# Wide fp32 products of a cross attention kernel as four strips of 32 columns, with a redrawn order of tasks

## The chip, the cores and the metric

The kernel runs on one core of one Trainium2 chip. The metric is the device time of one execution in microseconds (us); 602.05 us is the median of three runs before the change. The engines of the core are TensorE (PE; its weight loads are shown apart as PEld), VectorE (DVE), ScalarE (ACT), GpSimd (POOL) and SyncE (SP), which issues nearly all DMAs.

## The reference, cut to what matters

All arrays are fp32. `x` is (2, 2048, 640), the context (2, 128, 384): its first 124 tokens are text, the last 4 are `ca`.

```python
query = x @ Wq;  keyt = enc @ Wk;  valt = enc @ Wv           # enc: the first 124 tokens
hs = mha(query, keyt, valt)                                  # 8 heads of 80
ca_q1 = einsum('btc,th->bch', ca, Wq_ca)[:, indices, :]      # 384 rows, spread to 2048 by indices
ca_hs1 = mha(ca_q1, x, x)
ca_hs2 = mha(ca_hs1 @ Wq, ca @ Wk_ca, ca @ Wv_ca)
out = (hs + ca_hs2) @ Wout + b_out + x
```

## The kernel before, in words

The order of all work is made by a planner written in the kernel, the class `Desk`. Each piece of work is a Python generator (a task) that yields operations `Do(engine, fn, after, needs, ..., rank, mode)`. `Desk.run` keeps a clock for each engine. Among the operations whose events have come and whose rooms (PSUM banks, buffers) are free, it takes for each engine those that can start first, and of these the one with the lowest sum of rank, a correction of its task from the table `RANKS`, and `change(mode)`, a price for leaving the tiling in which TensorE is. `issue` then emits the instructions, and the planner's own durations (`START`, `DRAIN`, `DRAINS` for TensorE) advance the clock. The instructions are pinned in the order in which they were emitted. So the tables set the order of the program; they cost nothing at run time.

Most TensorE work passes through `Desk.matmul` (L212), which emits one instruction for each product, and `Desk.transpose` (L222). An fp32 product shows as two matmul records and two weight loads. TensorE works in these tilings, written rows*columns of the array:

- 128*128, whole: the wide products. `queries`, `queries_fast` with its inner task `chain`, and `plain` make the queries (`pq<-xt,wq_sb`, `pq<-x_sums,wq_sums` and kin) out of blocks of 512 rows of `x`; a second inner task named `chain`, in `text_out_fast`, multiplies by Wout (`po<-wout_sums,hs`, `po<-wout_sb,hs` and kin, 320 columns). Both use sums of blocks, so that seven block products stand for eight. Smaller ones: `pk`, `pv`, `pw`, `po<-w_sb,p2T`. The transposes (`pt_...`, `pm`) are whole too.
- 128*32, four strips side by side: `hidden` (`ph<-pT,vpad`, values by probabilities) and `contract` (`acc<-ea,y_sb`).
- 64*128: `text_scores` (`sc<-kmain,q`, `sc<-krest,rests`) and half of `yz_block` (`pyz`).
- 32*128, four row groups: the adapter's scores (`s<-zop,cop` for the maxima, `s<-cop,zop` for the exponentials).

Operations of the wide chains carry `mode=(P, P)`, `sc` carries `(64, P)`, `ph` carries `(P, 32)`; the others carry none, and their change costs nothing in the planner's choice. `idle_work` multiplies zeros at the start, 14 times.

Around the products: `softmax` takes the maxima of `sc` on VectorE (`m`), the exponentials on ScalarE (`p`), the division on POOL or VectorE, a block transpose on VectorE (`eb`), and a DMA round trip through HBM (`kept`, then `pT`). The adapter's maxima (`mx`) are on VectorE, its exponentials (`ea`) on ScalarE. Queries are read out of PSUM by ScalarE and VectorE (`q`), and each `po` is added to rows of `x` by VectorE (`x_more`, `last_rows`); `stored` sends these rows out, with the adapter's part added by an indirect DMA that POOL issues. There are 8 blocks of 512 rows and 16 units `m` of 256 rows.

In the chains a product waits for the read of the same PSUM bank before it: `yield Do("PE", product, ready + at, needs=needs, mode=(P, P))`, where `at` is the event of that read.

Of the kernel before, what the change touches and what calls it, by code (L numbers as in the profile page):

```python
# [14 lines left out]
P = 128  # L15
# [4 lines left out]
class Event:  # L20


    def __init__(self):
        self.t = None
# [33 lines left out]


class Task:  # L60
    def __init__(self, gen, rank, key, more):
        self.gen, self.rank, self.key, self.more, self.last = gen, rank, key, more, Event()


class Desk:
# [1 line left out]


    ENGINES = ("PE", "ACT", "DVE", "POOL", "SP", "NONE")
    WHOLE, SWITCH, LEAVE, ANOTHER = (P, P), 12.6, 12.9, -0.8  # L70
    START = {(P, P): 0.107, (64, P): 0.143, (P, 64): 0.107, (64, 32): 0.1, (P, 32): 0.03}
    DRAIN = {
        ((P, P), (32, P)): 0.136, ((P, P), (64, P)): 0.035, ((P, P), (P, 64)): 0.056, ((P, P), (P, 32)): 0.067,
        ((32, P), (P, 32)): 0.049, ((P, 64), (P, P)): 0.07, ((P, P), (P, P)): 0.0,
    }
    DRAINS = {(64, P): 0.172, (32, P): 0.108, (P, 32): 0.115}
    MORE = {
        "v_transpose": 0.025, "v_stream_shuffle": 0.09, "v_scalar_tensor_tensor": 0.07, "v_reciprocal": 0.035,
        "a_activation": 0.045,
# [3 lines left out]


    RANKS = {
        "adapter": {1: 0.3},
        "chain": {8: -11, 9: -18, 12: -2, 13: -1, 14: -17, 15: -5, 17: 4, 18: 4, 19: 8, 20: -6, 24: -15, 26: 6,
            27: 2, 37: -13, 38: 14, 39: 14, 40: 14, 41: 3, 45: 6, 50: 12, 51: 10, 52: -5, 57: -2, 62: 2, 65: -8,
            67: 0.1, 68: 0.1, 69: 0.1, 71: 11, 80: -12, 85: 9},
        "contract": {0: 4, 3: 8},  # L90
        "halves_away": {1: -6, 6: 7},
        "keys": {0: 4},
        "probabilities": {3: 7, 4: 1, 8: -4, 10: 4, 14: -0.5},
        "queries": {0: -2},
        "queries_fast": {4: 1},
        "residual": {14: -14},
        "rest_back": {8: 4, 9: 12, 10: -11},
        "second": {0: 1.6},
        "softmax": {12: -6, 19: 4, 21: 1, 22: 3, 23: -3, 24: 2, 26: -7, 27: -10, 28: 10},
        "stored": {7: -8},  # L100
        "sums_of_wq": {0: 4},
        "text_scores": {0: -2, 5: -2},
        "text_values": {0: 13},
        "values_weights": {0: 6},
        "wq_turned": {0: 2},
        "x_load": {1: -12, 6: -6},
        "y_rows": {1: 5, 3: 10, 4: 10, 7: 10},
        "yz_block": {0: -11, 1: -6, 5: 1.3, 6: 5, 7: 4.7},
    }

    def __init__(self, tc):
        self.tc, self.nc, self.now, self.spent, self.mode = tc, tc.nc, 0.0, 0.0, None
        self.free = {e: 0.0 for e in self.ENGINES}
        self.queue = {e: [] for e in self.ENGINES}
        self.events, self.landed, self.channel, self.log, self.begun = {}, 0.0, 0.0, [], {}

    def event(self, key):
        return key if isinstance(key, Event) else self.events.setdefault(key, Event())
# [2 lines left out]
        return self.event(key).t is not None  # L121

    def begin(self, gen, rank):
        name = gen.__name__
        n = self.begun[name] = self.begun.get(name, -1) + 1
        task = Task(gen, rank, (name, n), self.RANKS.get(name, {}).get(n, 0.0))
        task.last.t = self.now
        self.go_on(task, None)

# [16 lines left out]
    def change(self, mode):  # L146


        if mode is None or mode == self.mode:
            return 0.0  # L150
        return self.LEAVE if self.mode == self.WHOLE else self.SWITCH if mode == self.WHOLE else self.ANOTHER

    def order(self, op):
        return (op.order() if callable(op.order) else op.order) + op.task.more
# [55 lines left out]
        self.mode, self.idle = mode, False  # L210

    def matmul(self, out, lhsT, rhs, **kw):  # L212
        self.pin(self.nc.tensor.matmul(out, lhsT, rhs, **kw))  # L213
        n = 1
        for size in rhs.shape[1:]:
            n *= size
        self._mode(*lhsT.shape)
        at_once = (P // self.mode[0]) * (P // self.mode[1])
        one = lhsT.dtype == F32R
        self.spent += self.slow() * (1 if one else 2) * max(n / 1.2, 107) / 1e3 / at_once  # L220

    def transpose(self, out, in_, ident):  # L222
        self.pin(self.nc.tensor.transpose(out, in_, ident))
# [41 lines left out]
def kernel(  # L265
# [40 lines left out]
    desk = Desk(tc)  # L306
# [217 lines left out]
    def idle_work():  # L524

        zeros = sp.tile([P, P], F32, name="zeros")
        yield Do("DVE", lambda: desk.v_memset(zeros, 0.0), [])

        op = yield Do("NONE", lambda at: (bank(at[0], "unread"), at[0]), needs=[(banks, 1)])
        to, at = op.value
        for n in range(IDLE):

            def product():
                matmul(to[:, :P], zeros, zeros, start=True, stop=True)

            yield Do("PE", product, [] if n else [op.at], frees=[(banks, at)] if n == IDLE - 1 else [])

# [559 lines left out]
    def queries(n, after, first=False):  # L1099

        b, sb = divmod(n, NSB)
        yield Do("NONE", lambda: None, after)
        t, at = xt[b, sb]

        def room(s):
            q_of[n] = q_slot(s[0], f"q_{n}"), s[0]

        if first:
            yield Do("NONE", room, after, needs=[(qslots, 1)])
            q = q_of[n][0]  # L1110
            op = yield Do("NONE", lambda s: [bank(i, f"pq_{n}_{c}") for c, i in enumerate(s)], [], needs=[(banks, 3)])
            pq, three = op.value, op.slots[0]
            for i in range(NCH):

                def part(i=i):
                    for c in range(3):
                        matmul(
                            pq[c], wq_of(i, c), t[:, :, i, :], start=(i == 0), stop=(i == NCH - 1)
                        )

                op = yield Do("PE", part, [*after, ("wq", i)])
            for c in range(3):
                yield Fork(one(evacuate(q[:, c, :], pq[c], three[c], after=[op.at], marks=[("qc", n, c)])), 4)
        for c in range(3 if first else 0, NCH):

            def part(s, z=None, c=c):
                if z:
                    room(z)
                pq = bank(s[0], f"pq_{n}_{c}")
                for i in range(2):  # L1130
                    matmul(pq, wq_of(i, c), t[:, :, i, :], start=(i == 0), stop=False)
                return pq

            own = [(qslots, 1)] if n not in q_of else []
            op = yield Do("PE", part, [*after, "wq4"], needs=[(banks, 1), *own], mode=(P, P))
            pq, s, q = op.value, op.slots[0][0], q_of[n][0]

            for i0, i1 in ((2, 4), (4, NCH)):

                def part(c=c, i0=i0, i1=i1):  # L1140
                    for i in range(i0, i1):
                        matmul(pq, wq_of(i, c), t[:, :, i, :], start=False, stop=(i == NCH - 1))

                op = yield Do("PE", part, mode=(P, P))
            if c < 4:
                yield Fork(one(evacuate(q[:, c, :], pq, s, after=[op.at], marks=[("qc", n, c)], rank=0)), 0)
            else:
                yield Fork(halves_away(n, pq, s, op.at) if n else first_halves(pq, s, op.at), 0)
        used(b, sb, op)
        yield Do("NONE", lambda: None, [("qc", n, c) for c in range(4)], marks=[("q", n)])  # L1150
# [49 lines left out]
    def queries_fast(n, after):  # L1200
# [28 lines left out]
                if n + 1 == len(blocks):  # L1229
                    desk.event("last query").t = op.at.t  # L1230

        def chain(c, steps):

            po, s, at = None, None, []
            for k, ((x, y, plus), ready, (i, u)) in enumerate(steps):
# [19 lines left out]

                if x is not None:
                    needs = ([(banks, 1)] if k == 0 else []) + ([(qslots, 1)] if n not in q_of else [])
                    op = yield Do("PE", product, ready + at, needs=needs, mode=(P, P))
                    if k == 0:
                        po, s = op.value, op.slots[0][0]  # L1260
                    if n not in forked:
                        forked.add(n)
                        desk.event(("q slot", n)).t = desk.now
                        for c2 in (1, 2, 3):
                            yield Fork(chain(c2, chains[c2]), rank + 0.1 * c2)
                if plus:
                    op = yield Do("PE", fifth, [op.at] + at, mode=(P, P))
                counted(op, any(key[0] == "xs" for key in ready))
                yield from read(i, u, po, s, op.at, k == len(steps) - 1)
                at = [desk.event(("qr", n, i, u, len(begun_of[n, i, u]) - 1))]  # L1270
# [14 lines left out]
                    frees=frees, marks=marks, rank=0,  # L1285
                )), 0)

        yield Fork(chain(0, chains[0]), rank)
        yield Do("NONE", lambda: None, [("q slot", n)])
        yield from plain(n, t, NCH - 1, rank - 0.5, counted)  # L1290
        yield Do(
# [7 lines left out]
    def plain(n, t, c, rank, counted):  # L1299
# [4 lines left out]
                matmul(pq, wq_of(i, c), t[:, :, i, :], start=(i == 0), stop=False)  # L1304
            return pq

        op = yield Do("PE", part, needs=[(banks, 1)], mode=(P, P), rank=rank)
        pq, s = op.value, op.slots[0][0]
        for i0, i1 in ((2, 4), (4, NCH)):

# [1 line left out]
                for i in range(i0, i1):  # L1312
                    matmul(pq, wq_of(i, c), t[:, :, i, :], start=False, stop=(i == NCH - 1))

            op = yield Do("PE", part, mode=(P, P), rank=rank)
        counted(op, False)
        yield Fork(halves_away(n, pq, s, op.at), 0)

# [726 lines left out]
    def text_out_fast(m, rank):  # L2045
# [51 lines left out]
            (((s4, w[1][1], (0, 1)), [("hs", m, "s4")] + end_h, ((0, 1),)),),  # L2097
        )

        def chain(n, steps):  # L2100

            po, s, at = None, None, []
            for k, ((x, y, plus), after, ((i, u),)) in enumerate(steps):

                def product(s=None, k=k, x=x, y=y, plus=plus):
# [9 lines left out]
                    return to  # L2115

                op = yield Do(
                    "PE", product, after + at + ready, needs=[(banks, 1)] if k == 0 else [], mode=(P, P), rank=rank
                )
                if k == 0:  # L2120
                    po, s = op.value, op.slots[0][0]
# [15 lines left out]
                    yield Fork(stored(m, i, ends[m, i]), 1)  # L2137

        for n, steps in enumerate(chains):
            yield Fork(chain(n, steps), 30 + m)  # L2140

    fast_of, tile_left, ends = {}, {}, {}

# [109 lines left out]
```

## Time and profile before

| what | value |
|---|---|
| median of 3 runs | 602.05 us (601.88 to 604.86) |
| profiled execution: span from first to last instruction | 600.3 us |
| TensorE busy, matmul records | 583.0 us, 4535 |
| VectorE / ScalarE / POOL busy | 404.1 / 282.2 / 151.1 us |
| DMA moved | 113.55 MB, mean 189 GB/s |

The profile gives the profiled execution's span alone; the time that lies around it isn't recorded, and the median of the runs is 1.75 us above that span. Busy time is the union of an engine's instructions. Matmuls are pipelined and their ends are modelled, so that two records can overlap, and a TensorE that is busy can still stream with pauses: these show in the distance between starts. A row of the timeline merges instructions of one kind that follow each other: start, length, engine, line, operation, written tile<-read tiles, tiling or partitions, shape of the moving operand, number of records. The row of a stretch gives, for each engine, busy us and (in brackets) instructions, then the granted clock of TensorE, the DMA engines' share and GB/s. A row of the waits reads: who waited for whom, us in total, times, longest. A row of the groups gives busy us, mean ns of one, and the idle time ahead with what ended it.

### The profile page before, as it was taken

To read this page: it belongs to the slowest core of one execution; us is meant where nothing else is said; L and a number is where in the kernel's file an instruction comes from. 1 tells how busy PE (TensorE), PEld (TensorE's weight loads), DVE (VectorE), ACT (ScalarE), POOL (GpSimd) and SP (SyncE) were. 2 spreads that over 40 slices of the span, in tenths; PEclk is the share of its full clock that TensorE was granted. 3 is DMA by queue.
4 is the path that set the end of the run, shared out by engine and by line. 5 is a ranking of instruction groups with operands and counts; after the bars stand their busy time and mean duration, and the time that the engine had idled before them with its cause. 6 is when DMAs were issued, how large, how long until landed. Compare 5 with 4: busy or idle time off the path is not lost.

```text
span 600.3 us, 11804 instructions
## 1 busy us (share of the span) xinstructions
PE 583.0 (97%) x4535; PEld 363.2 (61%) x4535; DVE 404.1 (67%) x640; ACT 282.2 (47%) x770; POOL 151.1 (25%) x201
## 2 busy tenths in 40 slices
PE   9999989999999999999999999999999999999997
PEld 7575455756757655465666555666555557676664
DVE  2257698989999977464999999996422153344343
ACT  2233156455445499799844443345765741201010
POOL 7201021413215330004104443133112202062251
PEclk9999999999999999999999999999999999999999
DMA  8998825965969495454796999786943495799995
GB/s 278 176 238 161 153 80 166 178 178 172 137 170 212 136 184 179 150 161 141 189 265 193 258 216 277 227 218 183 241 128 79 101 255 125 231 217 285 231 236 160
DMA packets 152818, 113.55 MB, mean 189 GB/s; under 512 B 83253, under 2 KB 125621, under 8 KB 152762
## 3 DMA queue, kind: packets, MB, share of 16 engines
q1 hardware_dynamic: 147130, 102.11, 66.2%
q0 software_dynamic: 5632, 10.69, 10.2%
q8 instruction: 36, 0.59, 0.4%
q14 instruction: 20, 0.16, 0.1%
HBM read 71.89 MB, written 40.88 MB: 188 GB/s over the span
## 4 chain that ended last, share of the span: by engine, by line
PE 61%; DVE 23%; DMA 6%; ACT 6%; issue 3%; SPq 0%; DVEq 0%; ACTq 0%
PE po L213 23%; PE pq L213 11%; DVE mx L238 8%; PE acc L213 6%; PE ph L213 6%; DMA pT<-kept 5%; PE s L213 4%; DVE m L238 3%; ACT p L238 3%; PE sc L213 2%; ACT ea L238 2%; DVE eb L238 2%; PE pyz L213 2%; DVE q L238 2%; DVE zop L238 1%
## 5 line engine op out<-in xcount | busy, mean ns | idle before, releaser
L238 DVE TENSOR_REDUCE mx<-s 128x4 f32<-128x2048 f32 x48 | 109.2, 2276 | 6.2 <-PE s L213 6.2
L238 ACT ACTIVATE p<-sc,m 128x124 f32<-128x124 f32 x256 | 90.6, 385 | 31.3 <-DVE m L238 31.2
L238 ACT ACTIVATE ea<-s 128x2048 f32<-128x2048 f32 x48 | 91.3, 1903 | 26.9 <-PE s L213 26.8
L213 PE MATMUL pq<-xt,wq_sb 128*128 128x256 f32 (+1 forms) x272 | 86.1, 452 | 2.4 <-DVE q L238 2.3
L238 POOL TENSOR_TENSOR p<-p,r 128x992 f32<-128x992 f32 x19 | 35.5, 1869 | 203.7 <-DVE r L238 203.7
L213 PE MATMUL po<-wout_sums,hs 128*128 128x320 f32 x256 | 78.8, 440 | 0.0
L213 PE MATMUL po<-wout_sb,hs 128*128 128x320 f32 x240 | 75.0, 442 | 1.6 <-ACT p L238 1.3
L238 DVE TENSOR_TENSOR x_more<-x_more,po 128x320 f32<-128x320 f32 x72 | 34.3, 482 | 47.4 <-PE po L213 44.4
L213 PEld LDWEIGHTS pq<-xt,wq_sb 128*128 128x128 f32 x272 | 48.8, 190 | 27.0 <-issue 17.0
L213 PEld LDWEIGHTS po<-wout_sums,hs 128*128 128x128 f32 x256 | 46.7, 190 | 23.0 <-issue 5.4
L213 PEld LDWEIGHTS po<-wout_sb,hs 128*128 128x128 f32 x240 | 43.6, 189 | 25.9 <-issue 6.1
L238 DVE TENSOR_TENSOR last_rows<-last_rows,po 128x320 f32<-128x320 f32 x56 | 27.2, 486 | 46.0 <-PE po L213 45.6
L238 ACT ACTIVATION_READ_ACCUMULATOR p<-sc,m 128x1 f32 x256 | 58.0, 227 | 0.0
L238 ACT COPY hs<-ph 128x512 f32<-128x512 f32 (+1 forms) x34 | 18.5, 560 | 78.1 <-PE ph L213 78.1
L213 PE MATMUL acc<-ea,y_sb 128*32 128x384 f32 (+2 forms) x768 | 51.4, 385 | 0.0
L2003 POOL DMA_INDIRECT x_more<-o,query x18 | 28.1, 1560 | 91.7 <-DVE x_more L238 80.6
L238 DVE TENSOR_REDUCE m<-sc 128x4 f32<-128x496 f32 x64 | 40.3, 662 | 10.8 <-PE sc L213 10.8
L213 PE MATMUL ph<-pT,vpad 128*32 128x256 f32 x768 | 45.6, 381 | 1.2 <-DMA pT<-kept 1.0
L238 DVE STREAM_TRANSPOSE eb<-p 128x1024 f32<-128x1024 f32 x32 | 39.4, 1232 | 1.9 <-DMA kept<-eb 1.7
L213 PE MATMUL pq<-xt,wq 128*128 128x512 f32 x80 | 39.8, 612 | 0.0
L213 PEld LDWEIGHTS sc<-kmain,q 64*128 64x128 f32 x512 | 31.1, 187 | 12.8 <-issue 6.3
L213 PE MATMUL sc<-kmain,q 64*128 64x124 f32 x512 | 37.1, 284 | 0.0
(207 smaller groups left out, 787.1 us busy)
## 6 DMA issues: line engine op xcount, KB each, us to landing
kept<-eb SPq DMA_DIRECT2D x32, 512.0 KB
pT<-kept SPq DMA_DIRECT2D x64, 256.0 KB
landing<-away SPq DMA_DIRECT2D x60, 128.0 KB
xi<-in_x_dram SPq DMA_DIRECT2D x28, 256.0 KB
x_more<-in_x_dram SPq DMA_DIRECT2D x18, 320.0 KB
out_dram<-x_more SPq DMA_DIRECT2D x18, 320.0 KB
last_rows<-in_x_dram SPq DMA_DIRECT2D x14, 320.0 KB
out_dram<-last_rows SPq DMA_DIRECT2D x14, 320.0 KB
```

The lines of the kernel that those rows point to most:

```text
L213: self.pin(self.nc.tensor.matmul(out, lhsT, rhs, **kw))
L238: self.pin(getattr(engine, what)(*args, **kw))
L2003: desk.pin(nc.gpsimd.indirect_dma_start(out=t, out_offset=None, in_=o2_of[b], in_offset=bass.IndirectOffsetOnAxis(ap=query[:, st : st + 1] ...
```

## The change

`Desk.matmul` emits a product whose stationary operand has over 64 rows and over 64 columns as four products of 32 columns each, into the four quarters of the output's partitions. It stays whole while TensorE's tiling is 128*128, which now comes about through transposes and through the idle products (`Desk.warm`) alone, and lasts until an operation of another tiling follows. The wide operations carry `Desk.WIDE` instead of `(P, P)`; in `change` this counts as 128*128 when TensorE is in that tiling, and as 128*32 otherwise, the tiling that `ph` carries.

The planner's prices change: entering 128*32 (`SWITCH`) 18.4665 for 12.6, leaving it or 128*128 (`LEAVE`) -14.8473 for 12.9, any other change (`ANOTHER`) 39.005 for -0.8. Its durations for starts and drains change a little. `RANKS` is redrawn: its keys are now the leading whole-number arguments of a task's function instead of the count of tasks begun under that name, and it has entries for most tasks. The second `chain` is renamed `sums_chain`. No buffer, DMA, engine or arithmetic of a product changes apart from the split.

```diff
-    WHOLE, SWITCH, LEAVE, ANOTHER = (P, P), 12.6, 12.9, -0.8
-    START = {(P, P): 0.107, (64, P): 0.143, (P, 64): 0.107, (64, 32): 0.1, (P, 32): 0.03}
+    WHOLE, WIDE, SWITCH, LEAVE, ANOTHER = (P, 32), (P, None), 18.4665, -14.8473, 39.005
+    START = {(P, P): 0.06, (64, P): 0.107, (P, 64): 0.107, (64, 32): 0.03, (P, 32): 0.03}
...
-        "text_scores": {0: -2, 5: -2},
+        "text_scores": {(0,): 19, (1,): -6, (2,): -17.3, (3,): 1, (5,): -10, (6,): -1, (7,): -15.8, (9,): -14,
+            (12,): 6.7, (14,): 1.5, (15,): 5},
...
     def change(self, mode):
+        if mode == self.WIDE:
+            mode = self.mode if self.mode == (P, P) else self.WHOLE
         if mode is None or mode == self.mode:
             return 0.0
-        return self.LEAVE if self.mode == self.WHOLE else self.SWITCH if mode == self.WHOLE else self.ANOTHER
+        return self.LEAVE if self.mode in (self.WHOLE, (P, P)) else self.SWITCH if mode == self.WHOLE else self.ANOTHER
...
     def matmul(self, out, lhsT, rhs, **kw):
-        self.pin(self.nc.tensor.matmul(out, lhsT, rhs, **kw))
+        rows, cols = lhsT.shape
+        wide = rows > 64 and cols > 64 and self.mode != (P, P)
+        for c in range(0, cols, 32) if wide else (0,):
+            strip = slice(c, c + 32 if wide else cols)
+            self.pin(self.nc.tensor.matmul(out[strip], lhsT[:, strip], rhs, **kw))
...
-        self._mode(*lhsT.shape)
+        self._mode(rows, 32 if wide else cols)
...
+    def warm(self, out, zeros):
+        self.pin(self.nc.tensor.matmul(out, zeros, zeros, start=True, stop=True))
+        self._mode(P, P)
...
-                    op = yield Do("PE", product, ready + at, needs=needs, mode=(P, P))
+                    op = yield Do("PE", product, ready + at, needs=needs, mode=Desk.WIDE)
```

More of the change, by code (lines that the diff above doesn't have):

```diff
@@ L60, with __init__ @@
 class Task:
-    def __init__(self, gen, rank, key, more):
-        self.gen, self.rank, self.key, self.more, self.last = gen, rank, key, more, Event()
+    def __init__(self, gen, rank, more):
+        self.gen, self.rank, self.more, self.last = gen, rank, more, Event()
 class Desk:
     ENGINES = ("PE", "ACT", "DVE", "POOL", "SP", "NONE")
-    WHOLE, SWITCH, LEAVE, ANOTHER = (P, P), 12.6, 12.9, -0.8
-    START = {(P, P): 0.107, (64, P): 0.143, (P, 64): 0.107, (64, 32): 0.1, (P, 32): 0.03}
+    WHOLE, WIDE, SWITCH, LEAVE, ANOTHER = (P, 32), (P, None), 18.4665, -14.8473, 39.005
+    START = {(P, P): 0.06, (64, P): 0.107, (P, 64): 0.107, (64, 32): 0.03, (P, 32): 0.03}
     DRAIN = {
-        ((P, P), (32, P)): 0.136, ((P, P), (64, P)): 0.035, ((P, P), (P, 64)): 0.056, ((P, P), (P, 32)): 0.067,
-        ((32, P), (P, 32)): 0.049, ((P, 64), (P, P)): 0.07, ((P, P), (P, P)): 0.0,
+        ((P, P), (32, P)): 0.136, ((P, P), (64, P)): 0.095, ((P, P), (P, 32)): 0.093,
+        ((32, P), (P, 32)): 0.06, ((P, P), (P, P)): 0.0,
     }
-    DRAINS = {(64, P): 0.172, (32, P): 0.108, (P, 32): 0.115}
+    DRAINS = {(64, P): 0.148, (32, P): 0.108, (P, 32): 0.1}
     MORE = {
@@ L85 @@
     RANKS = {
[L86 to L101, printed above, removed]
-        "text_scores": {0: -2, 5: -2},
[L103 to L107, printed above, removed]
@@ L108 @@
-        "yz_block": {0: -11, 1: -6, 5: 1.3, 6: 5, 7: 4.7},
+        "adapter": {(1,): -11.4},
+        "chain": {(2, 0): 6, (2, 1): 10, (2, 2): -2, (2, 3): 19, (3, 0): -3, (3, 1): 21, (3, 2): -2, (3, 3): -2,
+            (4, 1): -1, (4, 2): -0.6, (5, 0): -6, (5, 1): 20, (5, 2): -4, (5, 3): 3, (6, 0): -1, (6, 1): 16,
+            (6, 3): -17, (7, 0): -3.1, (7, 1): -39.6, (7, 2): -4, (7, 3): -25},
+        "context": {(): -4},
+        "contract": {(0, 0): 5.7, (1, 0): -0.3, (1, 1): 5},
+        "first_halves": {(): 2},
@@ new lines @@
+        "first_loads": {(): 1},
+        "gather_rows": {(): -5},
+        "halves_away": {(1,): 0.7, (3,): -1.3, (4,): 10, (5,): -2, (7,): -5},
+        "keys": {(): 1.6},
+        "load_wout": {(): -13},
+        "probabilities": {(0,): 0.2, (1,): -4.7, (2,): -6, (3,): 7, (4,): 24.6, (5,): 11, (6,): 8.2, (7,): -23,
+            (8,): 21.5, (9,): 27.1, (10,): -19.8, (11,): 25.9, (12,): 3, (13,): 16, (14,): 24.8,
+            (15,): 24.7},
+        "queries": {(0,): 1, (1,): -0.1},
+        "queries_fast": {(2,): 36, (3,): -13, (4,): 20, (5,): 11.1, (7,): -19.7},
@@ new lines @@
+        "residual": {(1,): 20, (2,): -14, (3,): -1.7, (4,): -21, (5,): -8, (7,): -16, (8,): 3, (11,): 4, (13,): 15,
+            (14,): 5},
+        "rest_back": {(0,): 6, (1,): 20, (2,): -8.8, (3,): -10, (4,): 4, (5,): 38, (8,): 8, (10,): 10, (11,): -18.2,
+            (12,): -24, (13,): 7, (14,): 2, (15,): 0.7},
+        "second": {(0,): -25},
+        "softmax": {(0, 0): -17.3, (0, 1): -4, (1, 0): -9, (2, 0): -7, (5, 0): -12.7, (5, 1): -20, (6, 0): -1.6,
+            (6, 1): 2.1, (7, 0): -18, (7, 1): 4, (8, 0): -19, (9, 0): 8.6, (9, 1): 0.7, (10, 0): 28,
+            (10, 1): 6, (11, 0): -1, (11, 1): -11.7, (12, 1): -3, (13, 0): -4, (13, 1): 10, (14, 0): -1.4,
+            (15, 0): 10, (15, 1): -19},
@@ new lines @@
+        "stored": {(0, 0): 21, (0, 1): 12, (1, 0): -8, (1, 1): 7.2, (2, 1): 13, (3, 0): -6, (3, 1): -15, (4, 0): 2,
[3 rows of a table added]
+        "sums_chain": {(0, 0): -12.8, (0, 1): -4, (0, 2): 1, (0, 3): -2.3, (1, 0): -12, (1, 1): 20, (1, 2): 1.9,
[7 rows of a table added]
+        "sums_of_wout": {(): -2},
+        "sums_of_wq": {(): 2},
+        "text": {(1,): 7, (2,): -23, (3,): 12.8, (4,): 6, (5,): -10, (6,): 0.9, (7,): -1, (8,): -10, (9,): 2,
+            (11,): 2.5, (12,): 11.1, (14,): -20.7, (15,): -5},
+        "text_scores": {(0,): 19, (1,): -6, (2,): -17.3, (3,): 1, (5,): -10, (6,): -1, (7,): -15.8, (9,): -14,
+            (12,): 6.7, (14,): 1.5, (15,): 5},
@@ new lines @@
+        "text_values": {(): 17},
+        "values_weights": {(): 21},
+        "wq_turned": {(): 4.2},
+        "x_first": {(): 1},
+        "x_load": {(0, 2): -4.4, (1, 1): 16, (1, 2): -20, (1, 3): 11},
+        "y_rows": {(0, 0): 8, (0, 1): 16.8, (0, 2): -13, (0, 3): 34.1, (1, 0): 15, (1, 1): 8, (1, 2): -10,
+            (1, 3): -1},
+        "y_weights": {(): -6},
+        "yz_block": {(0, 0): -40, (0, 1): -21, (0, 2): -6, (1, 0): -0.5, (1, 1): -16, (1, 2): -17, (1, 3): -22},
+        "z_weights": {(): 4.9},
@@ L114, in __init__ @@
         self.queue = {e: [] for e in self.ENGINES}
-        self.events, self.landed, self.channel, self.log, self.begun = {}, 0.0, 0.0, [], {}
+        self.events, self.landed, self.channel, self.log = {}, 0.0, 0.0, []
     def event(self, key):
@@ L123, in begin @@
     def begin(self, gen, rank):
-        name = gen.__name__
-        n = self.begun[name] = self.begun.get(name, -1) + 1
-        task = Task(gen, rank, (name, n), self.RANKS.get(name, {}).get(n, 0.0))
+        frame, key = gen.gi_frame, []
+        for arg in frame.f_code.co_varnames[: frame.f_code.co_argcount]:
+            if type(frame.f_locals[arg]) is not int:
+                break
+            key.append(frame.f_locals[arg])
+        task = Task(gen, rank, self.RANKS.get(gen.__name__, {}).get(tuple(key), 0.0))
         task.last.t = self.now
@@ L216, in matmul @@
             n *= size
-        self._mode(*lhsT.shape)
+        self._mode(rows, 32 if wide else cols)
         at_once = (P // self.mode[0]) * (P // self.mode[1])
         one = lhsT.dtype == F32R
-        self.spent += self.slow() * (1 if one else 2) * max(n / 1.2, 107) / 1e3 / at_once
+        self.spent += self.slow() * (1 if one else 2) * max(n / 1.2, 107) / 1e3 / at_once * (4 if wide else 1)
+    def warm(self, out, zeros):
+        self.pin(self.nc.tensor.matmul(out, zeros, zeros, start=True, stop=True))
+        self._mode(P, P)
+        self.spent += self.slow() * 0.214
     def transpose(self, out, in_, ident):
@@ L535, in product @@
             def product():
-                matmul(to[:, :P], zeros, zeros, start=True, stop=True)
+                desk.warm(to[:, :P], zeros)
             yield Do("PE", product, [] if n else [op.at], frees=[(banks, at)] if n == IDLE - 1 else [])
@@ L1134, in queries @@
             own = [(qslots, 1)] if n not in q_of else []
-            op = yield Do("PE", part, [*after, "wq4"], needs=[(banks, 1), *own], mode=(P, P))
+            op = yield Do("PE", part, [*after, "wq4"], needs=[(banks, 1), *own], mode=Desk.WIDE)
             pq, s, q = op.value, op.slots[0][0], q_of[n][0]
@@ L1142, in part @@
                         matmul(pq, wq_of(i, c), t[:, :, i, :], start=False, stop=(i == NCH - 1))
-                op = yield Do("PE", part, mode=(P, P))
+                op = yield Do("PE", part, mode=Desk.WIDE)
             if c < 4:
@@ L1230, in counted, with chain @@
                     desk.event("last query").t = op.at.t
-        def chain(c, steps):
+        def chain(n, c, steps):
             po, s, at = None, None, []
@@ L1264, in chain @@
                         for c2 in (1, 2, 3):
-                            yield Fork(chain(c2, chains[c2]), rank + 0.1 * c2)
+                            yield Fork(chain(n, c2, chains[c2]), rank + 0.1 * c2)
                 if plus:
-                    op = yield Do("PE", fifth, [op.at] + at, mode=(P, P))
+                    op = yield Do("PE", fifth, [op.at] + at, mode=Desk.WIDE)
                 counted(op, any(key[0] == "xs" for key in ready))
@@ L1286, in read @@
                 )), 0)
-        yield Fork(chain(0, chains[0]), rank)
+        yield Fork(chain(n, 0, chains[0]), rank)
         yield Do("NONE", lambda: None, [("q slot", n)])
@@ L1305, in part @@
             return pq
-        op = yield Do("PE", part, needs=[(banks, 1)], mode=(P, P), rank=rank)
+        op = yield Do("PE", part, needs=[(banks, 1)], mode=Desk.WIDE, rank=rank)
         pq, s = op.value, op.slots[0][0]
@@ L1313, in part @@
                     matmul(pq, wq_of(i, c), t[:, :, i, :], start=False, stop=(i == NCH - 1))
-            op = yield Do("PE", part, mode=(P, P), rank=rank)
+            op = yield Do("PE", part, mode=Desk.WIDE, rank=rank)
         counted(op, False)
@@ L2098, in text_out_fast, with sums_chain @@
         )
-        def chain(n, steps):
+        def sums_chain(m, n, steps):
             po, s, at = None, None, []
@@ L2117, in chain @@
                 op = yield Do(
-                    "PE", product, after + at + ready, needs=[(banks, 1)] if k == 0 else [], mode=(P, P), rank=rank
+                    "PE", product, after + at + ready, needs=[(banks, 1)] if k == 0 else [], mode=Desk.WIDE, rank=rank
                 )
@@ L2139, in text_out_fast @@
         for n, steps in enumerate(chains):
-            yield Fork(chain(n, steps), 30 + m)
+            yield Fork(sums_chain(m, n, steps), 30 + m)
     fast_of, tile_left, ends = {}, {}, {}
```

10 rows, old and new, of the table RANKS are left out of this document.

## The prediction

> **What bounds the kernel now.** I read the page first (shares, slices, chain), then the stretches, then who makes TensorE wait, and last the order of TensorE's work at a few places.
>
> ```profile
> span 600.3 us, 11804 instructions
> PE 583.0 (97%) x4535; PEld 363.2 (61%) x4535; DVE 404.1 (67%) x640; ACT 282.2 (47%) x770; POOL 151.1 (25%) x201
> PE   9999989999999999999999999999999999999997
> DVE  2257698989999977464999999996422153344343
> PEclk9999999999999999999999999999999999999999
> PE 61%; DVE 23%; DMA 6%; ACT 6%; issue 3%; SPq 0%; DVEq 0%; ACTq 0%
> ```
>
> TensorE is busy for 583.0 of 600.3 us at the full clock, and it holds 61% of the chain that ended last; VectorE holds 23%. So the time is a sum of TensorE's work, with stretches in which VectorE leads.
>
> ```profile
> core 0: us, PE busy (x) PEld busy (x) DVE busy (x) ACT busy (x) POOL busy (x), PEclk, DMA share, GB/s
> 120.00:210.00 90.00, 86.31 (x588) 59.24 (x586) 87.33 (x115) 45.67 (x173) 26.73 (x23) 1.00 0.71 167
> 210.00:285.00 75.00, 73.46 (x817) 41.76 (x813) 45.00 (x73) 68.63 (x156) 10.62 (x16) 1.00 0.60 163
> 285.00:405.00 120.00, 114.94 (x928) 73.07 (x920) 116.90 (x142) 56.90 (x223) 34.67 (x27) 1.00 0.89 230
> 405.00:495.00 90.00, 89.82 (x956) 50.02 (x955) 34.16 (x72) 55.28 (x59) 18.33 (x16) 1.00 0.65 164
> 495.00:596.00 101.00, 101.00 (x603) 67.80 (x601) 42.15 (x90) 12.04 (x25) 27.89 (x18) 1.00 0.88 217
> ```
>
> From 120 to 210 and from 285 to 405 us VectorE is as full as TensorE (87.33 of 90, 116.90 of 120); from 405 on it is idle for more than half of the time, and there TensorE alone sets the pace. TensorE's own idle time is small:
>
> ```profile
> PE pq L213 <- DVE q L238: 5.0, 6, 1.6
> PE s L213 <- ACT ea L238: 1.4, 4, 0.7
> PE po L213 <- ACT p L238: 1.3, 1, 1.3
> ...
> PE po L213 <- DVE hs L238: 0.2, 1, 0.2
> ```
>
> Twelve such rows, the first three and the last shown, add up to 12.7 us. But a busy TensorE isn't one that streams without pause. How much a change of tiling costs is read from the distance between starts:
>
> ```profile
> 48.27 0.86 PE L213 MATMUL pvca<-w_vca,caT 128*32 128x160 f32 x20
> 49.07 1.88 PE L213 MATMUL pv<-w_v,ctxT 128*128 128x320 f32 x6
> ...
> 480.73 1.07 PE L213 MATMUL acc<-ea,y_sb 128*32 128x384 f32 x16
> 481.73 1.34 PE L213 MATMUL po<-wout_sb,hs 128*128 128x320 f32 x4
> 483.00 0.56 PE L213 MATMUL s<-cop,zop 32*128 32x128 f32 x8
> 483.49 1.07 PE L213 MATMUL acc<-ea,y_sb 128*32 128x256 f32 x16
> 484.49 1.34 PE L213 MATMUL po<-wout_sums,hs 128*128 128x320 f32 x4
> ...
> 583.48 2.80 PE L213 MATMUL ph<-pT,vpad 128*32 128x256 f32 x48
> 586.21 2.42 PE L213 MATMUL po<-wout_sb,hs 128*128 128x320 f32 x8
> 588.47 0.70 PE L213 MATMUL po<-wout_sb,wout_sums 128*128 128x320 f32 x2
> 589.01 1.24 PE L213 MATMUL po<-wout_sb,hs 128*128 128x320 f32 x4
> 590.08 0.70 PE L213 MATMUL po<-wout_sb,wout_sums 128*128 128x320 f32 x2
> ```
>
> An fp32 product leaves two records. In whole tiling, four of 320 columns take 590.08 - 589.01 = 1.07 us, 0.269 each over longer runs. The eight at 586.21 follow a change and take 588.47 - 586.21 = 2.26, which is 8 x 0.269 + 0.107: starting whole costs 0.107 us. The four at 481.73 take 1.27 until the 32-row products start, 0.194 over 4 x 0.269: start and exit of a whole stretch together. In 128*32 tiling four strips run side by side, so 48 records are 12 packs. The 48 at 583.48 take 2.73 until the next start and the sixteen at 483.49, 4 packs of 256 columns too, take 1.00. Two equations: a pack costs (2.73 - 1.00) / 8 = 0.216 us, and 2.73 - 12 x 0.216 = 0.139 is left for start and exit of a strip stretch.
>
> **The change, part by part.**
>
> Steady products. A pack of four strips costs 0.216 us for 256 columns; a whole record costs 0.269 for 320, which is 0.215 for 256. The strips of the wide products take the lengths that whole products have now (256, 320, 512), so their stream costs what it does today. Bounds: nothing below, and above 0.001 us for each of the 1,050 records that would become packs, 1 us. I take 0. (1,050 is a count over TensorE's order of records, 1,262 wide ones less 212 that follow a transpose without another tiling between.) The `ph` strips also show two strips reading the same moving rows at this rate, since each head has two halves; four that read the same rows aren't shown.
>
> Start and exit. Counted in the same order, 98 stretches are whole and hold no transposes; the first is at 49.07 and the last at 586.21. As strips each costs 0.139 for 0.194, so 98 x 0.055 = 5.4 us go. Exits to 64-row products behave alike, and after 32-row products both entries are nearly free.
>
> Boundaries that vanish. At 49 places such a stretch touches one of 128*32 strips, first at 49.07 and last at 586.21. There one start and exit fall away: 49 x 0.139 = 6.8 us.
>
> New boundaries. Where wide products stand between others and transposes, strips must now give way to whole: some 6 new places at 0.139, 0.8 us back.
>
> `warm` gives the idle products in the form they had: 0. Evacuation, semaphores, VectorE, ScalarE, POOL and SP carry the same instructions; a group of products ends at the same time in either form, and the readers wait for its last record.
>
> Instructions. 1,050 records more than triple: 3,150 more, 7,690 in all if the order stayed, and as many weight loads. The loads lie beside the products:
>
> ```profile
> 519.46 5.39 PE L213 MATMUL ph<-pT,vpad 128*32 128x256 f32 x96
> 519.46 4.91 PEld L213 LDWEIGHTS ph<-pT,vpad 128*32 128x32 f32 x96 [0.44 <-DVE x_more L238]
> L213 PEld LDWEIGHTS ph<-pT,vpad 128*32 128x32 f32 x768 | 23.6, 110 | 19.4 <-issue 3.3 <-DVE x_more L238 2.0 <-DMA x_more<-in_x_dram 0.4
> q8 instruction: 36, 0.59, 0.4%
> ```
>
> 96 loads of 110 ns end with 96 products in 5.39 us. The 36 packets of q8 fit TensorE's 9,070 records, 252 to a packet. A strip stretch of 320 columns would use a packet up in 252 / 8 x 0.269 = 8.5 us; the stretch from 210 to 285 uses one in 252 / 1630 x 75 = 11.6 with no sign of hunger. I take 0. Without that cover some 61 packets, 1.07 us each (0.4% of sixteen engines' span over 36), would be exposed: 65 us at most.
>
> With the order kept: 5.4 + 6.8 - 0.8 = 11.4 us.
>
> The order. Every rank is redrawn and the weights for a change too: from a wide stretch a score product (`sc`) is now preferred by 14.8, from any other tiling it is put back by 39 against 18.5 for a wide product, and `ph` counts as wide. No row of before shows the new order. On the good side it can win back at most TensorE's 12.7 us of waits; on the bad side it can starve VectorE (priced below). I take 5 us of gain, under half of the waits: wide work may now fill a hole between contractions without a switch, and 32 of the 49 vanishing boundaries lie from 210 to 285 and from 405 to 495, where VectorE isn't full.
>
> Sum: 600.3 - 11.4 - 5 = 583.9. The median of the runs, 602.05, is 1.75 above the profiled span (lowest run 601.88). With that: 585.6.
>
> [...] The row: in 128*32 tiling the loads of a pack run beside its products (above). [...]
>
> **The rivals.**
>
> VectorE holds the gain back. 44 of the 98 stretches and 6 of the 49 boundaries lie in the two stretches where VectorE is 97% full: 44 x 0.055 + 6 x 0.139 = 3.3 us. If these stay as long as they are and the new order brings nothing: 602.05 - (11.4 - 3.3) = 594. For it: the waits on `q`. Against: TensorE can take work forward from the later stretches.
>
> The order gives more. If all waits go and 25 of the 96 or so entries from wide work into 32-row products go with them (25 x 0.139 = 3.5): 602.05 - 11.4 - 12.7 - 3.5 = 574. Against it: each score piece has one bank group and waits for its reader.
>
> The order starves VectorE: slower. Place: the two full stretches, which hold 87.33 + 116.90 = 204.2 us of VectorE's work in 210. Mechanism: after a 32-row product a wide one now goes ahead of a ready `sc`, whose maxima and exponentials feed VectorE. At 90% share the stretches take 226.9, 16.9 more, and 8.1 is still won elsewhere: 611. It turns slower by 0.5% below a share of 0.924. Against: in these stretches 24 stretches of 64-row products stand among 44 wide and 39 32-row ones, and from wide ones `sc` is now preferred.
>
> Loads not hidden. If the load of a wide strip did wait, at 0.110 for each pack: 1,050 x 0.110 = 115 us, 701. Against: the `ph` rows. [...]
>
> No change. The new order spends the 11.4 us on more changes of tiling (82 more at 0.139): 602.
>
> **How the numbers follow.** A measurement of this kernel tells about 0.5%, 3 us, from no change. Forecast 585.6 (578 to 592 as its own range): 0.45. Held back, 594: 0.20. More, 574: 0.18. No change, 602: 0.07. VectorE starved, 611: 0.08. Loads exposed, 701: 0.02. Faster by over 0.5%: 0.45 + 0.20 + 0.18 = 0.83; within 0.07; slower 0.10. The range 574 to 598 leaves out the last three and half of the low case's tail, about 2 in 10.
>
> **What the next profile would show.** About 7,700 matmul records, mostly 128*32, whole wide ones only beside transposes. Packs of wide strips 0.269 us apart at 320 columns, 0.216 at 256; if 0.32 or more, the loads are exposed. `ph` and `po` next to each other without a hole. PE's waits near 8 us. VectorE's full stretches no longer than 210 us together. The last stretch (495 on, 101 us, 4 wide stretches and 7 boundaries) shorter by about 1.2 us for the same work. Wrong would be: packs slower than whole records, as many changes of tiling as now, or VectorE under 92% between its first and last score maxima.

## The result, and the profile after

The changed kernel takes 588.24 us (median of 4 runs, 586.4 to 589.56) against 603.45 for the kernel before in the same runs: ratio 0.9742, 95% interval 0.9703 to 0.9781. The forecast was 585.6. The span of the profiled execution fell from 600.3 to 586.5 us, by 13.8.

The page after: its shares, VectorE's row of slices, the chain, and the queue that brings instructions:

```profile
span 586.5 us, 18596 instructions
PE 571.5 (97%) x7913; PEld 301.2 (51%) x7913; DVE 403.7 (69%) x642; ACT 279.1 (48%) x764; POOL 153.2 (26%) x205
DVE  2257789999999665487889999976366354444443
PE 78%; DVE 9%; DMA 5%; ACT 5%; issue 2%; POOL 0%; SPq 0%; DVEq 0%; ACTq 0%
q8 instruction: 62, 1.02, 0.8%
```

TensorE now holds 78% of the chain for 61%, VectorE 9% for 23%. The work of VectorE is the same (403.7 for 404.1 us) but lies elsewhere, as the stretches show:

```profile
120.00:210.00 90.00, 87.93 (x1286) 50.26 (x1286) 82.25 (x106) 51.16 (x181) 40.47 (x39) 1.00 0.79 171
210.00:285.00 75.00, 72.76 (x1139) 38.95 (x1139) 49.78 (x72) 62.98 (x151) 1.29 (x1) 1.00 0.50 144
285.00:405.00 120.00, 117.08 (x1656) 59.17 (x1652) 106.51 (x134) 52.28 (x161) 38.75 (x35) 0.99 0.89 229
405.00:495.00 90.00, 89.58 (x1308) 48.93 (x1311) 44.91 (x89) 57.92 (x119) 18.73 (x14) 1.00 0.84 214
```

From 285 to 405 us VectorE is busy for 106.51 of 120 where it was 116.90, from 120 to 210 for 82.25 of 90 where it was 87.33; from 405 to 495 it has 44.91 for 34.16. TensorE's own waits, the first and the last of ten rows:

```profile
PE pt_p L269 <- DVE p2pad L284: 1.7, 2, 1.4
...
PE s L254 <- DVE zop L284: 0.2, 1, 0.2
```

They add up to 9.6 us for 12.7 (the prediction had about 8). In the timeline of TensorE the strips run as forecast:

```profile
530.87 1.26 PE L254 MATMUL po<-wout_sb,hs 128*32 128x320 f32 x16
531.95 0.72 PE L254 MATMUL po<-wout_sb,wout_sums 128*32 128x320 f32 x8
532.49 2.77 PE L254 MATMUL ph<-pT,vpad 128*32 128x256 f32 x48
535.08 4.49 PE L254 MATMUL po<-wout_sb,hs 128*32 128x320 f32 x64
539.38 4.49 PE L254 MATMUL po<-wout_sums,hs 128*32 128x320 f32 x64
```

Sixteen records of 320 columns, four packs, take 531.95 - 530.87 = 1.08 us, sixteen packs 539.38 - 535.08 = 4.30: 0.269 each, what a whole record took. The 48 of `ph` take 535.08 - 532.49 = 2.59 for 2.73 before, 12 x 0.216 with nothing left over: start and exit are gone on both sides. Over the whole trace the median distance of packs is 0.216 us at 256 columns and 0.269 at 320, the same as of whole records before.

### The profile page after: what moved, and what is told of

It reads as the page before. It is cut to its first block, busy times and chain, and to the rows that moved or that the text cites. A ratio compares the mean times of both kernels' runs of the same rounds, so it can differ in the third digit from the quotient of the medians.

```text
span 586.5 us, 18596 instructions
## 1 busy us (share of the span) xinstructions
PE 571.5 (97%) x7913; PEld 301.2 (51%) x7913; DVE 403.7 (69%) x642; ACT 279.1 (48%) x764; POOL 153.2 (26%) x205
## 4 chain that ended last, share of the span: by engine, by line
PE 78%; DVE 9%; DMA 5%; ACT 5%; issue 2%; POOL 0%; SPq 0%; DVEq 0%; ACTq 0%
PE po L254 24%; PE pq L254 24%; PE ph L254 6%; PE sc L254 5%; PE s L254 5%; PE acc L254 5%; DMA kept<-eb 4%; PE pyz L254 2%; ACT ea L284 2%; DVE mx L284 2%; ACT p L284 2%; DVE eb L284 1%; PE pv L254 1%; PE pk L254 1%; DVE zop L284 1%
## 5 line engine op out<-in xcount | busy, mean ns | idle before, releaser
L254 PE MATMUL pq<-xt,wq_sb 128*32 128x256 f32 (+2 forms) x974 | 83.7, 428 | 0.0
L254 PE MATMUL po<-wout_sums,hs 128*32 128x320 f32 (+1 forms) x988 | 77.0, 433 | 0.0
L254 PE MATMUL po<-wout_sb,hs 128*32 128x320 f32 x944 | 76.0, 433 | 0.1
L284 POOL TENSOR_TENSOR p<-p,r 128x992 f32<-128x992 f32 x16 | 29.9, 1866 | 121.7 <-DVE r L284 121.7
L254 PEld LDWEIGHTS pq<-xt,wq_sb 128*32 128x32 f32 (+1 forms) x974 | 35.6, 113 | 34.4 <-issue 18.9
L254 PEld LDWEIGHTS po<-wout_sb,hs 128*32 128x32 f32 x944 | 32.7, 111 | 32.6 <-issue 1.6
L254 PEld LDWEIGHTS po<-wout_sums,hs 128*32 128x32 f32 (+1 forms) x988 | 32.9, 111 | 31.9 <-issue 1.0
L254 PE MATMUL ph<-pT,vpad 128*32 128x256 f32 x768 | 47.7, 386 | 0.0
L2049 POOL DMA_INDIRECT x_more<-o,query x16 | 24.6, 1540 | 71.5 <-DVE x_more L284 40.5
L2049 POOL DMA_INDIRECT last_rows<-o,query x16 | 25.0, 1562 | 64.5 <-DVE last_rows L284 43.3
L254 PEld LDWEIGHTS sc<-kmain,q 64*128 64x128 f32 x512 | 31.6, 187 | 15.5 <-issue 9.7
```

The lines of the kernel that those rows point to most:

```text
L254: self.pin(self.nc.tensor.matmul(out[strip], lhsT[:, strip], rhs, **kw))
L284: self.pin(getattr(engine, what)(*args, **kw))
L2049: desk.pin(nc.gpsimd.indirect_dma_start(out=t, out_offset=None, in_=o2_of[b], in_offset=bass.IndirectOffsetOnAxis(ap=query[:, st : st + 1] ...
```

## Experiments

**Strips and order apart.** Two kernels split the change. In the first the planner of before decides as it did, and only the emission makes strips:

```diff
 # kernel before
-        self.pin(self.nc.tensor.matmul(out, lhsT, rhs, **kw))
+        rows, cols = lhsT.shape
+        wide = rows > 64 and cols > 64 and self.tiled != (P, P)
+        for c in range(0, cols, 32) if wide else (0,):
+            strip = slice(c, c + 32 if wide else cols)
+            self.pin(self.nc.tensor.matmul(out[strip], lhsT[:, strip], rhs, **kw))
+        self.tiled = ...   # the real tiling, beside self.mode, which stays as the planner had it
```

> The order of before, product for product, with the wide products as four strips except next to transposes. Theory S (the gain is starts, exits and vanished boundaries of the tiling): 98 x 0.055 + 49 x 0.139 - 0.8 = 11.4 us less than before, ratio 0.981, and whole-to-strip holes gone at the 49 boundaries. Theory V (VectorE's full stretches keep their length): 8.1 us less, ratio 0.987. Theory O (the gain is the redrawn order): ratio 1.00.

Measured: 598.84 us, ratio 0.9935 (0.9907 to 0.9964), span 596.9. The strips alone give 3.4 us of span in the old order, 3.9 by the ratio. Neither theory S (11.4) nor V (8.1) has that size; O (nothing) is out too.

The second is the changed kernel, planner and all, with whole emission:

```diff
 # changed kernel
-        for c in range(0, cols, 32) if wide else (0,):
-            strip = slice(c, c + 32 if wide else cols)
-            self.pin(self.nc.tensor.matmul(out[strip], lhsT[:, strip], rhs, **kw))
+        self.pin(self.nc.tensor.matmul(out, lhsT, rhs, **kw))
```

> The order of the changed kernel, product for product, but every wide product whole. In the changed kernel's trace 109 wide stretches are strips and 68 times such a stretch touches other 128*32 products. Theory S: 109 x 0.055 + 68 x 0.139 - 0.7 (5 boundaries to transposes gone) = 14.8 us more than the changed kernel, so 603, ratio to before 1.00. Theory O: like the changed kernel, ratio 0.975 to 0.98. If part is the order's own, the ratio lies between.

Measured: 601.57 us, ratio 0.9973 (0.9944 to 1.0002), span 598.0. So theory S's side holds: by the ratio the new order by itself can't be told from no change. The spans are 600.3 (neither), 596.9 (strips), 598.0 (order) and 586.5 (both): 3.4 and 2.3 us alone, 13.8 together (by the ratios 3.9 and 1.6 alone, 15.5 together). More than half of the gain needs both.

A span is that of one execution, and executions differ in their clock. By the clock records of the profiled ones the full clock is granted 6.66 us after the start of the span before, 4.33 with the strips, 7.15 with the order alone and 6.00 after. With the strips TensorE is 0.85 us ahead at 8 us, before the first strip, so of their 3.4 us 0.85 isn't theirs. The new order with whole products took 599.19 to 599.7 us in its three executions with a granted clock of 0.999 or more, below each of the 33 such executions of the kernel before (600.76 to 604.46); its other nine, at 0.990 to 0.995, hide that.

Why, the page of the second shows, first its shares and then its chain:

```profile
PE 585.2 (98%) x4535; PEld 363.2 (61%) x4535; DVE 405.4 (68%) x642; ACT 279.5 (47%) x764; POOL 152.5 (25%) x205
PE 86%; DVE 6%; ACT 3%; issue 1%; DMA 1%; SPq 1%; DVEq 0%; ACTq 0%
```

With whole products the new order is bound by TensorE nearly throughout (86% of the chain): VectorE's load is spread, but TensorE changes tiling more often (68 boundaries between wide and other 128*32 work for 49). The strips take just that away. In the old order they speed up an engine that must wait. The busy time of TensorE and the sum of its waits tell the two orders apart. With strips the busy time falls by 10.1 us in the old order (583.0 to 572.9) and by 13.7 in the new (585.2 to 571.5), near theory S's 11.4 and 14.8. But the waits grow from 12.7 to 19.2 us in the old order, and only from 8.0 to 9.6 in the new. The same instructions of both old-order kernels, before first, then strips, show where:

```profile
69.81 0.51 PE L213 MATMUL s<-zop,cop 32*128 32x512 f32 x4
75.86 1.02 ACT L238 CAST krest<-k_parts 128x992 fp32r<-128x992 f32 x1
83.90 0.68 DVE L238 COPY q<-pq 128x512 f32<-128x512 f32 x1
84.63 1.13 PE L213 MATMUL pq<-xt,wq_sb 128*128 128x256 f32 x4 [1.59 <-DVE q L238]
208.45 0.51 PE L213 MATMUL s<-cop,zop 32*128 32x384 f32 x8
583.48 0.85 PE L213 MATMUL ph<-pT,vpad 128*32 128x256 f32 x12
```

```profile
68.06 0.50 PE L218 MATMUL s<-zop,cop 32*128 32x512 f32 x4
76.70 1.02 ACT L245 CAST krest<-k_parts 128x992 fp32r<-128x992 f32 x1 [2.58 <-DMA k_parts<-k_away]
84.75 0.67 DVE L245 COPY q<-pq 128x512 f32<-128x512 f32 x1
85.48 0.85 PE L218 MATMUL pq<-xt,wq_sb 128*32 128x256 f32 x12 [3.64 <-DVE q L245]
88.35 1.77 PE L218 MATMUL sc<-kmain,q 64*128 64x124 f32 x16
210.49 0.51 PE L218 MATMUL s<-cop,zop 32*128 32x384 f32 x8
580.25 1.05 PE L218 MATMUL ph<-pT,vpad 128*32 128x256 f32 x16
```

At 68 us the strips lead by 1.75. Then TensorE waits 3.64 us for VectorE's `q` in place of 1.59, and the lead is a lag of 0.85. VectorE's copy `q` is late by the same 0.85 (84.75 for 83.90), and so is ScalarE's `krest` ahead of it (76.70 for 75.86), which waits for a DMA round trip through HBM (`k_parts`, sent back at 72.3 us for 70.6). Why SyncE issued it later isn't shown. After that the clock falls (granted 0.62 on average from 85.5 to 90 us): `sc` of 16 records takes 1.77 us for 1.16 elsewhere, and at 208 us the lag is 2.04. From 120 to 210 us next to nothing is won, with VectorE 87 of 90 us busy in both. Only from there to the end 2.04 turns into a lead of 3.23. The stretches of the strips in the old order, with the clock ahead of DMA's share:

```profile
75.00:120.00 45.00, 40.88 (x540) 20.53 (x532) 37.73 (x54) 21.36 (x83) 11.43 (x10) 0.96 0.52 134
120.00:210.00 90.00, 85.09 (x1250) 45.17 (x1250) 87.35 (x113) 46.72 (x181) 26.98 (x21) 1.00 0.71 169
210.00:285.00 75.00, 71.99 (x1079) 38.14 (x1071) 46.94 (x75) 67.98 (x150) 11.63 (x19) 1.00 0.62 169
285.00:405.00 120.00, 113.95 (x1597) 61.16 (x1593) 115.63 (x143) 58.00 (x227) 35.74 (x27) 1.00 0.91 232
```

TensorE's longest wait row grows from 5.0 to 8.1 us, and its waits for ScalarE's `ea` from 1.4 to 2.7:

```profile
PE pq L218 <- DVE q L245: 8.1, 7, 3.6
PE s L218 <- ACT ea L245: 2.7, 8, 1.0
```

**Strips in the chains of `po` alone, old order.** A flag set around the `matmul` of the second chain lets only these products be strips.

> The order of before, strips in the chains of the output product (po) alone; queries stay whole. Theory H (in the old order VectorE and ScalarE hold what the query strips win, and the long wait at 82 us with the half clock after it costs 4 us): as fast as the strips everywhere in that order, or faster, 597 to 599, with nothing won before 330 us and no fall of the clock. Rival (strips of queries win as much as those of po): half of that gain is gone, 600.5.

Measured: 598.26 us, ratio 0.9938 (0.9912 to 0.9963). As theory H has it: with strips in fewer places the kernel is as fast as with all of them. In the profiled execution instructions common to both keep before's times within about 0.1 us from 8 to 338 us, there is no fall of the clock, and the gain of 4.4 us comes in the rest. So in that order the query strips win nothing on top.

**Halves of 64 columns.** The loop's 32 becomes 64, in either order. This keeps a shorter start (start and exit 0.150 us, whole 0.197, strips 0.137) and takes the vanished boundaries away.

> The order of before, with wide products as two products of 64 columns. No boundary can vanish, since 128*64 is a tiling of its own. If the length of the weight load sets the start of a stretch (110 ns at 32 columns, 190 at 128), the start lies between: 98 stretches save up to 0.04 us each, ratio 0.993 to 1.00. If any tiling in columns starts as strips do, 0.055 each, 5.4 us, ratio 0.991. If two halves stream slower than one whole, slower than before.

Measured: 601.77 us, ratio 0.9994 (0.9966 to 1.0021). By the ratio nothing clear of noise is won, though a stretch of halves did start and leave faster. In the timeline of this kernel:

```profile
480.40 1.07 PE L218 MATMUL acc<-ea,y_sb 128*32 128x256 f32 x16
481.40 1.30 PE L218 MATMUL po<-wout_sums,hs 128*64 128x320 f32 x8
482.63 1.07 PE L218 MATMUL acc<-ea,y_sb 128*32 128x128 f32 x16
```

Four packs take 1.23 until the strips start, 4 x 0.269 + 0.154, where whole needed 0.194. The profiled execution, at full clock, does span 597.8 us, 2.4 less than before, but 0.8 of that again came ahead of the first stretch of halves. It kept its lead through the wait on `q` (1.67 us, at 83.61). In eight of the twelve executions the granted clock was 0.993 to 0.997, and these took 601.13 to 605.16 us. What held the rest of the expected gain back isn't shown.

> The order of the changed kernel, wide products as two of 64 columns. In the old order's trace a stretch of halves starts and leaves for 32-row products in 0.150 us (whole 0.197, strips 0.139), yet halves moved the time by nothing there. Theory R (the new order lets TensorE's pauses count): against the whole form, 601.6, the starts give 109 x 0.047 = 5.1 us, so 596.5, and the 68 vanished boundaries make the other 9.5 us down to the strips' 588.2 or less. Rival, starts never count and the boundaries alone do: 601.6.

Measured: 597.03 us, ratio 0.9916 (0.9882 to 0.9949); 596.5 was worked out. In the new order the ratios go 0.9973 whole, 0.9916 halves, 0.9742 strips: 3.4 us by the starts (5.1 expected) and 10.5 by the boundaries (9.5 and the rest of the starts, 1.2). The profiled executions split it as 5.0 and 6.5 (spans 598.0, 593.0, 586.5), the first two at full clock and the last with one half clock of 3.41 us in it. Each part is known to some 2 us only; the sum, 11.5 to 13.9 of 14.8, is nearly the full price of the pauses.

**No whole products next to transposes, new order.** The split no longer asks for the tiling.

> The changed kernel, order kept, but wide products are strips also next to transposes (134 whole records less). 17 times wide work follows transposes directly and 10 times it goes over into them: (17 + 10) x 0.13 = 3.5 us more, less 5 exits, so 591.5, ratio 0.980 to 0.982. Rival: these stretches lie in the front, where other work hides them: 588.

Measured: 591.14 us, ratio 0.9806 (0.9774 to 0.9838), 0.0064 or 3.9 us over the changed kernel's 0.9742; 3.5 was expected. The two intervals just touch, but the lowest of the six runs (590.44) lies above the highest of the changed kernel (589.56). So keeping 134 records whole beside transposes is part of the gain.

**Without the corrections.** `RANKS = {}` in either kernel.

> The changed kernel with an empty table of corrections, all prices and durations of the planner as changed. Theory S with the order neutral: strips as in the changed kernel, order drawn by the prices alone, 588 to 595, ratio 0.975 to 0.985. If the corrections carry the order's part: over 600, with more waits of TensorE or VectorE less full between 120 and 405 us.

> The kernel before with an empty table of corrections; it stands beside the changed kernel without its table (642 us). If the strips and the new prices are what made that one slow, this one is near 605 to 615. If the tables repair what the planner's durations get wrong in either kernel, it is slow too, 620 to 650.

Measured: the changed kernel 642.47 us, ratio 1.0606 (1.055 to 1.0662); the kernel before 620.38, ratio 1.0301 (1.0265 to 1.0336). Both are slow, so the tables carry the order in either kernel: some 54 us in the changed one (642.5 against 588.2), 19 in the one before. With empty tables the changed planner is worse than the one before. Its waits of TensorE add up to 51.6 us (24.1 in the kernel before without its table), and the two longest rows are for VectorE:

```profile
PE po L199 <- DVE last_rows L229: 16.6, 4, 9.8
PE s L199 <- DVE mx L229: 13.3, 7, 5.0
```

**The clock.** In the changed kernel TensorE waits twice near 310 us (1.27 us until 309.67, 1.35 until 312.86), and then the clock stands at a half. The middle row below has 0.50:

```profile
308.00:313.20 5.20, 2.58 (x35) 2.07 (x27) 5.06 (x11) 2.53 (x5) 2.48 (x3) 1.00 0.63 153
313.30:316.60 3.30, 3.30 (x30) 1.22 (x28) 3.30 (x4) 1.10 (x3) 0.50 (x1) 0.50 0.64 159
316.70:320.00 3.30, 3.30 (x56) 1.64 (x56) 2.98 (x5) 2.13 (x10) 1.60 (x3) 1.00 1.01 212
```

First, idle products ahead of the transposes of `p2pad`:

```diff
             pt = bank(s[0], f"pt_p2_{b}")
+            for _ in range(6 if b == 0 else 0):
+                desk.pin(nc.tensor.matmul(pt[:, :P], ident, ident, start=True, stop=True))
```

> The changed kernel with six idle products (whole, 128 columns) ahead of the first transposes of p2pad, where TensorE waits for 1.35 us at 311 us and the clock then stands at a half from 313.2 to 316.6. Theory C (the wait lets the clock fall): the clock stays at 1.00 in most executions, 1.7 us less, 586.5, ratio 0.971. Rival: the window falls elsewhere or the idle products come too late; like the changed kernel, 0.974 to 0.977.

Measured: 587.51 us, ratio 0.974 (0.971 to 0.977): the rival. The idle products came too late. They began at 312.10 us, and the clock stood at a half from 312.28 on: twelve records took 314.68 - 312.10 = 2.58 us until the transposes, 0.215 each. The idle products at the start of the changed kernel, whole and of 128 columns too, begin 0.213 us apart before the full clock is granted at 6.00 us and 0.11 apart after it.

```profile
312.10 2.79 PE L1777 MATMUL pt_p<-ident 128*128 128x128 f32 x12
314.68 0.85 PE L269 MATMUL pt_p<-ident,p2pad 128*113 128x128 f32 x3
```

In this execution it had also fallen at 264.5 us, right after a wait of 1.23. Then two more such places:

> The changed kernel with idle products at three waits of TensorE instead of one: 4 ahead of the exponentials' scores at 264.7 us (wait 1.22), 5 ahead of the scores at 309.7 (1.27), 6 ahead of the transposes of p2pad. With the third alone the clock still fell, at 264.5 and at 312.3 us, for 3.413 us each. Theory C (short waits close together let the clock fall, and filling them keeps it up): no fall between 10 and 570 us, two halves of 3.4 us saved against that execution, 583.8 to 586.5, ratio 0.968 to 0.972. Rival: the clock falls for another reason, or the fills cost what they save: 0.974.

Measured: 588.09 us, ratio 0.9763 (0.9742 to 0.9785). The clock stood at one from 5.5 to 585.8 us, and the time is still not lower. Two of the three fills filled nothing, since they write the banks that the waiting products wait for, and they put their own 1.1 and 1.3 us ahead of these products:

```profile
PE sc L1856 <- DVE q L284: 1.3, 1, 1.3
PE s L1651 <- ACT ea L284: 1.2, 1, 1.2
```

L1856 and L1651 are the idle products themselves. So whether filling the waits keeps the clock up stays open. What the falls cost is seen in the changed kernel's four runs: granted clock 0.999, 0.998, 0.997, 0.992 with 586.4, 588.23, 588.24, 589.56 us.

No version beat the changed kernel beyond its interval.

## Why the prediction was right, and where it was not

- **Steady products**: right. 0.269 us a pack at 320 columns and 0.216 at 256, also with four strips that read the same moving rows.
- **Start and exit, boundaries, in themselves**: right. Stretches of wide strips between 64- or 32-row products start and leave in 0.137 us (median of 31 in the old order, 0.139 forecast; halves 0.150, whole 0.197), and boundaries cost nothing (2.59 for 2.73). In the trace of before exits are alike (whole stretches behind 32-row products: 0.197 us to 64-row, 0.199 to 32-row ones, medians of 12 and 15). Entries after 32-row products cost about 0.01 there: packs of 512 columns give way after 0.436 us to whole products and after 0.438 to strips (medians of 30 and 6), where whole records of 512 columns are 0.429 apart; at 16 entries into strips it is 0.06.
- **"With the order kept: 11.4 us"**: wrong. It measured 3.4 of span. The step took every pause of TensorE for time of the kernel. The pauses went (10.1 us of busy time), but 6.5 us of waits came in their place. VectorE holds two stretches, as the rival said. But between 68 and 208 us one wait behind VectorE and the clock cost 3.8 (from a lead of 1.75 to a lag of 2.04). And in 210 to 285, where ScalarE was 68.63 of 75 us busy, the strips won 0.5 us in place of 2.8 (the lag at the same 32-row products goes from 2.04 at 208 us to 1.49 at 287); there TensorE's waits for `ea` grew from 1.4 to 2.5. The rival's 8.1 passed over both. From 495 us on, where TensorE alone sets the pace, the strips won 1.2, just as forecast (a lead of 2.25 at 497 us, of 3.47 at 595).
- **"The order ... I take 5 us"**: wrong as a term. By itself the order is worth 2.3 us of span, by the ratio not clear of nothing; with the strips it is worth 596.9 - 586.5 = 10.4. The terms don't add up: each was costed at the other's absence.
- **New boundaries at transposes, 0.8 us**: the place was right, and avoiding more of them is worth 3.9.
- **Instructions**: right. q8 has 62 packets (61 forecast), TensorE 7,913 records (7,690 forecast for the old order), and packs keep their distance. The loads of a wide pack (0.111 us each) lie beside its products, since a pack takes no longer than a whole record did (0.269 us at 320 columns): the 64 loads of the `po` strips at 539.38 us take 4.17 us, and the next stretch starts 4.31 after them.
- **VectorE starved**: the condition came about, the price didn't. In the two stretches VectorE is busy for 82.25 + 106.51 = 188.8 of 210 us, a share of 0.90 for 0.97. The rival priced that share at 611 us and saw a slowdown below 0.924. The price took VectorE's work there as fixed; but it is spread to other stretches (405 to 495: 44.91 for 34.16), and the kernel is faster. Nor was a VectorE under 92% between its first and last score maxima a sign of being wrong: the share is 0.88 before and 0.82 after (from the first `m` to the last). That this room lets the strips' gain through fits the waits in the two orders, but no run tests it alone.

So the total, 13.8 us of span for a forecast of 16.4, fell within the range by luck: two errors of opposite sign, 8 us too much for the strips and 5.4 too little for the order on top of them (10.4 for 5).

## What to carry to other kernels

A pause of the busiest engine is worth its length only in stretches where that engine ends last (in the old order 10.1 us of TensorE's busy time went, and 3.4 of the span); with the order kept, go through the stretches and ask for each which engine is full, ScalarE too. A cheaper instruction form and a new order can each be worth little and together much: run the form in the old order and the order with the old form before the gain is put down to either. Where neighbouring work shared a tiling, the boundary cost nothing here (the 48 records of `ph` between strips took 2.59 us, 12 x 0.216, for 2.73 between whole products), and splitting wide fp32 products to get there was free, since a pack streamed at the whole product's rate (0.269 us at 320 columns).

## What the runs showed of the hardware

In these runs the clock fell to a half after waits that look short. In the strips in the old order TensorE idles for 3.64 us and then runs at a clock of 0.50 for 3.41 us (clock records of the trace). It fell after shorter waits too: in the run with one fill at 312.28 us, where the last wait, 1.26, had ended at 310.33, and in the changed kernel at 313.20, where the last, 1.35, had ended at 312.86. The new order with whole products had the same two waits (1.3 us each) and no fall, nor had the kernel before one after its wait of 1.59 us at 84 us. So the length of the wait alone doesn't decide; what does stays open. The clock records of the changed kernel have the full clock for 307.20 us, a half for 3.413, then the full clock for 269.65: 307.20 is 90 times the length of the fall and 269.65 is 79 times, within 0.03 us. Why isn't shown. The changed kernel's four executions, with a granted clock of 0.992 to 0.999, didn't all fall alike.

In these kernels a stretch of wide products between other tilings starts and leaves faster the fewer columns a product has: 0.197 us at 128 columns, 0.150 at 64, 0.137 at 32 (medians over the stretches between 64- and 32-row products in the three old-order kernels). The weight loads shorten with the columns as well (190 ns at 128, 110 at 32); that they are the cause isn't shown.
